# A recurrence's attention by halves of the batch, with its B and C projections as seven block products made with states on the partitions

## The chip, the cores and the metric

The kernel runs on one core of a Trainium2 chip, in one launch, in fp32. The metric is the device time of the whole kernel in microseconds (us), the lower the better. The core's engines work side by side and wait for each other through semaphores: TensorE (PE; its weight loads are listed as PEld), VectorE (DVE), ScalarE (ACT), GpSimd (POOL) and SyncE (SP), which here issues the transfers between DRAM and the on-chip memory SBUF. Matmuls write into PSUM, which has eight banks of 512 fp32 columns on 128 partitions.

## The reference

The kernel is a decoder of twelve stages over x of 4 sequences x 256 tokens x 256 channels. Each stage replaces x by the layer norm of x plus what the stage returns. The change lies in the seventh, a recurrence with 24 heads, 64 states and 64 channels per head (Di = 1536):

```python
x = hidden_states * rsqrt(mean(hidden_states ** 2, -1) + eps) * norm_w
xz = x @ in_proj_w.T + in_proj_b                  # 256 -> 2 x 1536
x, z = xz[..., :Di], xz[..., Di:]
x = silu(conv(x, conv_w) + conv_b)                # four taps, each channel by itself
xp = (x @ x_proj_w.T + x_proj_b).reshape(Bsz, L, H, 1 + 2 * S)
dt, Bs, Cs = xp[..., 0], xp[..., 1:1 + S], xp[..., 1 + S:]
Bs, Cs = (t / max(norm(t, axis=-1), 1e-12) for t in (Bs, Cs))
A_decay = exp(clip(A_log, -2.3, -0.01) * softplus(dt))
def step(carry, xs):                              # over the 256 tokens
    u_red = B_t * x_t.mean(-1)
    pe = mean(((1.0 - a_t) * u_red) ** 2, -1)
    boost = relu(tanh(beta * pe / (surprise_ema + 1e-06)))
    alpha = clip(alpha_base + (1.0 - alpha_base) * boost, 0.01, 0.999)
    h = alpha * h + (1.0 - alpha) * (B_t[..., None] * x_t[:, :, None, :])
    y = einsum('bhs,bhsd->bhd', C_t, h)
out = (Y * silu(z)) @ out_proj_w.T + out_proj_b   # 1536 -> 256
return hidden_states + res_gate * out
```

The eighth stage is a cross attention whose keys (`dca_keys`) do not depend on x; its queries (`dca_start`) do. The ninth rounds its weights, which `round_bits` does ahead of time in pieces.

## The kernel before

`run_ssd` (from L1281) computes the recurrence. A framework's scheduler turns the Python program into one queue per engine and sets the semaphores; an engine takes its instructions in the order of its queue, and a tile of a pool with n buffers comes free when its last reader has ended. `K.tt`, `K.ts`, `K.stt` and `K.reduce` are VectorE operations (L116, L125 and their neighbours), `K.ptt` is GpSimd's (L128), `K.act` ScalarE's (L131), `K.mm` TensorE's matmul (L137); `K.copy` takes VectorE and ScalarE by turns. An fp32 matmul is two passes in the profile's counts.

*In-projection* (`for f in range(2 * SDC)`). After the RMS norm and its transposes into `K.xT` (channels on partitions, 1024 tokens in columns), 24 chunks of 128 channels: two matmuls of 512 columns for each of two halves. Chunks 0 to 11 are copied by ScalarE into `xin`, with three columns of zeros ahead of each sequence, and convolved by VectorE: one `ts` and three `stt` of 128x1024, then SiLU into `xcT`. Chunks 12 to 23 go through SiLU into `YT`, the gates.

*Twelve pairs of heads.* `project(p)` makes B and C of a pair for eight tiles of 128 tokens: twelve matmuls each, with `xcT` as the stationary operand and 256 weight columns of `xw` moving. So tokens come out on partitions; VectorE adds the bias `xb` on the way from PSUM to `xp`. Pair 0 takes 24 columns more, the dt of all heads, from which `decays` makes `om`, one minus the decay. After each tile a step of the generator `attend(p - 1)` is put between, so that the attention of one pair lies between the products of the next:

- the squares of `xp` summed to `ss`, the reciprocal norms `rn`, the inputs transposed to `xt` (tokens on partitions), then some twelve small VectorE operations on `al` (alpha for 128 tokens x 16), and one tanh on ScalarE. GpSimd scales `xt` by (1 - alpha) x rn and the C half of `xp` by rn;
- alpha is transposed (`aT`), written to DRAM (`ad`) and read back on all partitions (`ap`, the buffer of `K.xT`): SP issues both;
- 16 transposes of `xp` (L1488) give BT and CT with states on partitions;
- for each two sequences, running products of alpha (`decay`, L1503, scans of 256 or 128 columns per sequence and head), scores C B^T (`sc`, `sd`), their product with the decays, values with `xt`, and the product with the gates in `YT`.

After each token tile one piece of `round_bits` goes between as well (`bits`).

*End.* `sums` (out-projection, twelve matmuls per token tile) of tiles 0 to 3 run beside the last pair's attention and `add` forms x; then come `dca_keys`, the sums of tiles 4 and 5, and `dca_start`, which has the sums and adds of tiles 6 and 7 put between its steps (`parts`).

Of the kernel before, what the change touches and what calls it, by code (L numbers as in the profile page):

```python
# [810 lines left out]
def small_heads_T(K, dst, src, col, chunks, scales=None, tp=None):  # L811


    ps = (tp or K.tp).tile([P, 4, P], F32, name="ps", tag="tp")
    for c in range(chunks):
        K.nc.tensor.transpose(ps[:, c, :], src[:, c * P : (c + 1) * P], K.ident)
    if scales is None:
        K.copy(dst[:, :, col : col + P], ps[:, 0:chunks, :])
    else:
        for lo, hi, g, b in scales:  # L820
            K.copy_scaled(dst[:, :, col + lo : col + hi], ps[:, 0:chunks, lo:hi], g, b)
# [451 lines left out]
def load_ssd(K, wp):  # L1273
    return {
        "cols": K.load(wp, "l2a_cols", [P, 86]),
        "rows": K.load_rows(wp, "l2a_rows"),
        "o": K.load(wp, "l2a_wo", [P, SDC, D], "(c p) n -> p c n", p=P),
    }


def run_ssd(K, w, more):  # L1281
    nc, tc = K.nc, K.tc
    N = B * L
    cols, rows = w["cols"], w["rows"]
    norm_w, in_b, conv_w, conv_b = cols[:, 0:2], cols[:, 2:26], cols[:, 26:74], cols[:, 74:86]
    dt_b, a_log, l2ab, l2beta, ema = (rows[:, SH * k : SH * (k + 1)] for k in range(5))
    out_b, res = rows[:, 120:376], rows[:, 376:377]
    by_b = lambda ap: ap.rearrange("p (b l) -> p b l", l=L)
    with ExitStack() as ctx:
        one = ctx.enter_context(tc.tile_pool(name="ssd1", bufs=1))  # L1290
        YT = one.tile([P, SDC, N], F32, name="YT")
        om = one.tile([P, NT, SH], F32, name="om")
        ab = one.tile([P, SH], F32, name="ab")
        nab = one.tile([P, SH], F32, name="nab")
        bse = one.tile([P, SH], F32, name="bse")


        cx = ExitStack()
        xcT = cx.enter_context(tc.tile_pool(name="ssdx", bufs=1)).tile([P, SDC, N], F32, name="xcT")
        with ExitStack() as c0:  # L1300
            c0.enter_context(K.turns())
            w0 = c0.enter_context(tc.tile_pool(name="ssd0", bufs=2))
            ws = c0.enter_context(tc.tile_pool(name="ssdw", bufs=6))
            pm = c0.enter_context(tc.tile_pool(name="ssdm", bufs=4, space=PSUM))
            xn = w0.tile([P, NT, D], F32, name="xn", bufs=1)
            ss = w0.tile([P, NT], F32, name="ss", bufs=1)
            for b in range(B):
# [5 lines left out]
                ps = K.tp.tile([P, DC, L], F32, name="ps", tag="tp")  # L1313
# [6 lines left out]
            for f in range(2 * SDC):  # L1320
                wi = ws.tile([P, DC, P], F32, name="wi")
                nc.sync.dma_start(out=wi, in_=K.A["l2a_in"][f])
                if f < SDC:
                    xin = w0.tile([P, B, L + 3], F32, name="xin")
                    nc.gpsimd.memset(xin[:, :, 0:3], 0.0)
                for h in range(2):
                    s = slice(512 * h, 512 * h + 512)
                    ps = pm.tile([P, 512], F32, name="ps")
                    for c in range(DC):
                        K.mm(ps, wi[:, c, :], K.xT[:, c, s], c == 0, c == DC - 1)  # L1330
                    if f < SDC:
                        K.act(xin[:, 2 * h : 2 * h + 2, 3 : L + 3], by_b(ps), AF.Identity, bias=in_b[:, f : f + 1])
                    else:
                        K.act(YT[:, f - SDC, s], ps, AF.Silu, bias=in_b[:, f : f + 1])
                if f < SDC:
                    acc = w0.tile([P, B, L], F32, name="acc")
                    cw = [conv_w[:, 4 * f + j : 4 * f + j + 1] for j in range(4)]
                    K.ts(acc, xin[:, :, 3 : L + 3], cw[3], conv_b[:, f : f + 1], MUL, ADD)
                    for j in range(3):
                        K.stt(acc, xin[:, :, j : j + L], cw[j], acc, MUL, ADD)  # L1340
                    K.act(by_b(xcT[:, f, :]), acc, AF.Silu)

        gb = one.tile([P, D], F32, name="gb")
        K.ts(gb, out_b, res, None, MUL)

        def sums(i, ps, lo, hi):
            for k in range(lo, hi):

                K.mm(ps, YT[:, k, i * P : (i + 1) * P], w["o"][:, k, :], k == 0 and i % 2 == 0, k == SDC - 1 and i % 2 == 1)
# [6 lines left out]
        with ExitStack() as c1:  # L1356
            c1.enter_context(K.turns(1))
            w1 = c1.enter_context(tc.tile_pool(name="ssda", bufs=1))
            w2 = c1.enter_context(tc.tile_pool(name="ssdb", bufs=2))
            ws = c1.enter_context(tc.tile_pool(name="ssdxw", bufs=3))  # L1360
            px = c1.enter_context(tc.tile_pool(name="ssdpx", bufs=2, space=PSUM))
            dram = c1.enter_context(tc.tile_pool(name="ssdad", bufs=2, space=bass.MemoryType.DRAM))
            pc = c1.enter_context(tc.tile_pool(name="ssdpc", bufs=1, space=PSUM))
            py = c1.enter_context(tc.tile_pool(name="ssdpy", bufs=1, space=PSUM))

            def decays(dt, wd):

                z = wd.tile([P, NT, SH], F32, name="z")
                e = wd.tile([P, NT, SH], F32, name="e")
                K.tt(z, dt, again(dt_b, NT), ADD)  # L1370
                K.act(e, z, AF.Abs)
                K.act(e, e, AF.Exp, scale=-1.0)
                K.act(e, e, AF.Ln, bias=K.eps[1.0])
                K.stt(z, z, 0.0, e, MAX, ADD)
                t = wd.tile([P, SH], F32, name="t")
                K.ts(t, a_log, -2.3, -0.01, MAX, MIN)
                K.tt(z, z, again(t, NT), MUL)
                K.act(z, z, AF.Exp)
                K.ts(om, z, -1.0, 1.0, MUL, ADD)
                K.ts(t, l2ab, -3.32, -0.015, MAX, MIN)  # L1380
                K.act(nab, t, AF.Exp, scale=LN2)
                K.ts(ab, nab, -1.0, 1.0, MUL, ADD)
                t = wd.tile([P, SH], F32, name="t")
                K.ts(t, l2beta, -2.0, 2.0, MAX, MIN)
                K.act(bse, t, AF.Exp, scale=LN2)
                t = wd.tile([P, SH], F32, name="t")
                K.ts(t, ema, 1e-6, None, ADD)
                nc.vector.reciprocal(t, t)

                K.stt(bse, bse, 1.0 / SD**3, t, MUL, MUL)  # L1390

            def project(p, rest=iter(()), beside=iter(()), bits=iter(())):


                n = 2 * P + (SH if p == 0 else 0)
                half = []
                for k in range(2):
                    xw = ws.tile([P, 6, n], F32, name="xw", padded_shape=[P, 6, 2 * P + SH])
                    nc.sync.dma_start(out=xw[:, :, 0 : 2 * P], in_=K.A["l2a_xw"][p, k])
                    if p == 0:  # L1400
                        nc.sync.dma_start(
                            out=xw[:, :, 2 * P : n],
                            in_=K.A["l2a_dt"][6 * P * k : 6 * P * (k + 1), :].rearrange("(c p) n -> p c n", p=P),
                        )
                    half.append(xw)
                xb = w2.tile([P, 2 * P], F32, name="xb")
                nc.sync.dma_start(out=xb, in_=K.A["l2a_xb"][p : p + 1, :].to_broadcast([P, 2 * P]))
                xp = w2.tile([P, NT, 2 * P], F32, name="xp")
                for i in range(NT):
                    ps = px.tile([P, 512], F32, name="ps")  # L1410
                    for k in range(SDC):
                        K.mm(ps[:, 0:n], xcT[:, k, i * P : (i + 1) * P], half[k // 6][:, k % 6, :], k == 0, k == SDC - 1)
                    K.tt(xp[:, i, :], ps[:, 0 : 2 * P], xb, ADD)
                    if p == 0:
                        nc.scalar.copy(dt[:, i, :], ps[:, 2 * P : n])
                    for _ in rest:
                        pass
                    next(beside, None)
                    next(bits, None)
                return xp  # L1420

            def attend(p, xp):

                hs = slice(2 * p, 2 * p + 2)

                ss = w2.tile([P, NT, 4], F32, name="ss")
                for h in range(2):
                    sq = w1.tile([P, 4, 4, SD], F32, name="sq")
                    v = xp[:, 4 * h : 4 * h + 4, :]
                    K.act(sq.rearrange("p i g s -> p i (g s)"), v, AF.Square)  # L1430
                    K.reduce(ss[:, 4 * h : 4 * h + 4, :], sq, ADD)
# [6 lines left out]
                for h in range(2):  # L1438
                    ps = K.tp.tile([P, 4, P], F32, name="ps", tag="tp")
                    for k in range(4):  # L1440
                        i = 4 * h + k
                        nc.tensor.transpose(ps[:, k, :], xcT[:, p, i * P : (i + 1) * P], K.ident)
# [1028 lines left out]
```

## Time and profile before

| | us |
|---|---|
| median of 3 runs (2395.62 to 2405.2) | 2399.39 |
| the profiled execution's own time | 2403.96 |
| its span, first to last instruction | 2402.2 |
| TensorE busy in it | 2227.1 (93%) |
| VectorE busy | 1461.9 (61%) |
| ScalarE busy | 787.2 (33%) |
| GpSimd busy | 260.4 (11%) |

The mean granted clock of TensorE was 0.947. The recurrence takes about a third of the span. By stretches, with the busy time of each engine:

| stretch (us) | what runs | length | PE | DVE | ACT | POOL |
|---|---|---|---|---|---|---|
| 1009.2 to 1055 | in-projection, convolved chunks | 45.8 | 42.57 | 41.75 | 27.36 | 0.99 |
| 1055 to 1101 | in-projection, gates | 46.0 | 44.93 | 15.09 | 24.13 | 0.22 |
| 1101 to 1704.7 | twelve pairs | 603.7 | 602.39 | 280.96 | 80.98 | 53.16 |
| 1704.7 to 1789.5 | keys, sums, begin of the queries | 84.8 | 82.02 | 53.15 | 17.82 | 16.63 |

A busy share is a mean over such stretches: what an operation costs depends on whether something waits for it where it stands. A row of the timeline shown below has the start in us, the duration in us, the engine, the line, the operation, output <- inputs, sizes (partitions x elements) and how many instructions it joins; square brackets hold the idle time ahead of it and what ended it. A row of a group has the busy time of all, the mean in ns of one, and the idle time ahead of them with what ended most of it.

### The profile page before, as it was taken

The page shows a single profiled execution, that of the slowest core. Times are in us where ns is not written, and L with a number is a line of the kernel's source. Part 1 is how long each engine was busy: PE and PEld are TensorE (multiplying, and loading weights), DVE is VectorE, ACT ScalarE, POOL GpSimd, SP SyncE. Part 2 cuts the span into 40 slices and gives each one's busy share as a digit, 9 for nine tenths or more (in the row PEclk, how much of TensorE's full clock was granted, in tenths as well). Part 3 has the DMA queues.
Part 4 walks back from the last instruction along what each step waited for, and adds up shares of the span by engine and source line. Part 5 has one row for each costly group of instructions (what it writes and reads, how often), then busy time and mean ns, then how long its engine had stood idle before and what let it go on. Part 6 is the DMA issues. An engine that isn't in the chain of part 4 may idle for free. (4 is left out here: it accounts for less than half of the span.)

```text
span 2402.2 us, 28595 instructions
## 1 busy us (share of the span) xinstructions
PE 2227.1 (93%) x10504; PEld 1516.5 (63%) x10504; DVE 1461.9 (61%) x3178; ACT 787.2 (33%) x1763; POOL 260.4 (11%) x419
## 2 busy tenths in 40 slices
PE   8899998589987999899999999999999988899998
PEld 4566763335434655536888888888776545477676
DVE  4999975999876121380465544445565658686466
ACT  5677765223432011261211111111122223253443
POOL 1000010220010322200101000110110001200001
PEclk9999998788987999999999999999998888999999
DMA  7222221222213644220222111111100021100000
GB/s 224 62 55 60 48 66 31 56 70 53 49 36 94 195 129 125 77 72 5 75 86 87 47 47 56 66 47 49 48 22 1 1 77 43 42 1 1 1 1 18
DMA packets 133747, 139.50 MB, mean 58 GB/s; under 512 B 13892, under 2 KB 121766, under 8 KB 131944
## 3 DMA queue, kind: packets, MB, share of 16 engines
q1 hardware_dynamic: 133608, 137.68, 20.0%
q8 instruction: 83, 1.36, 0.2%
q14 instruction: 56, 0.46, 0.1%
HBM read 134.79 MB, written 2.85 MB: 57 GB/s over the span
## 5 line engine op out<-in xcount | busy, mean ns | idle before, releaser
L137 PE MATMUL ps<-xw,xcT 128*128 128x256 f32 (+1 forms) x2304 | 518.9, 382 | 0.3 <-ACT YT L131 0.3
L137 PEld LDWEIGHTS ps<-xw,xcT 128*128 128x128 f32 x2304 | 430.8, 190 | 64.0 <-issue 1.9
L116 DVE TENSOR_TENSOR xp<-ps,xb 128x256 f32<-128x256 f32 x96 | 40.5, 422 | 232.1 <-PE ps L137 232.0
L137 PE MATMUL sc<-kT,qT 32*128 32x256 f32 (+2 forms) x768 | 167.5, 412 | 10.0 <-DVE qn L134 9.7
L131 ACT ACTIVATE dA<-delta,negA 128x255 f32<-128x255 f32 x256 | 118.5, 501 | 131.1 <-DVE s L535 129.4
L137 PE MATMUL ssmps<-s,idz 128*128 128x512 f32 x256 | 143.7, 670 | 17.1 <-DVE s L116 16.0
L535 DVE TENSOR_TENSOR_SCAN s<-dA,s 128x512 f32<-128x512 f32 x128 | 154.6, 1219 | 2.6
L137 PEld LDWEIGHTS sc<-kT,qT 32*128 32x128 f32 (+1 forms) x768 | 106.9, 204 | 73.4 <-issue 45.2
L116 DVE TENSOR_TENSOR hT<-u,a 128x512 f32<-128x512 f32 x48 | 33.2, 691 | 186.0 <-PE u L137 184.9
L131 ACT ACTIVATE sq<-xp 128x1024 f32<-128x1024 f32 x24 | 25.4, 1057 | 314.1 <-DVE xp L116 314.1
L174 POOL TENSOR_SCALAR rstd<-mv 128x2 f32<-128x2 f32 x48 | 11.6, 241 | 951.9 <-DVE mv L166 932.7
L134 DVE TENSOR_REDUCE qn<-sc 128x2 f32<-128x480 f32 (+1 forms) x192 | 87.2, 506 | 39.1 <-PE sc L137 38.1
L131 ACT ACTIVATE e<-sT 128x512 f32<-128x512 f32 x128 | 70.9, 590 | 112.0 <-PE sT L137 109.9
L137 PE MATMUL sT<-q,kT 32*128 32x256 f32 (+1 forms) x384 | 103.4, 518 | 3.4 <-ACT e L131 3.3
L1503 DVE TENSOR_TENSOR_SCAN dec<-xT,idz 128x256 f32<-128x256 f32 (+1 forms) x192 | 89.8, 537 | 19.0 <-DMA xT<-ad 19.0
L131 ACT ACTIVATE a<-g 128x512 f32<-128x512 f32 x48 | 28.7, 599 | 206.4 <-PE g L137 206.4
L137 PE MATMUL g<-xT,wj 128*128 128x512 f32 x192 | 92.1, 603 | 0.7 <-ACT rows L105 0.7
L137 PE MATMUL u<-xT,wj 128*128 128x512 f32 x192 | 90.9, 595 | 0.0
L137 PEld LDWEIGHTS y<-wj,hT 128*128 128x128 f32 x384 | 73.0, 190 | 26.6 <-issue 18.2
L116 DVE TENSOR_TENSOR s<-du,bc 128x512 f32<-128x512 f32 x128 | 87.7, 694 | 2.7 <-PE ssmps L137 2.5
L137 PE MATMUL ps<-xT,wi 128*128 128x512 f32 x192 | 85.7, 603 | 4.0 <-ACT xin L131 4.0
L137 PE MATMUL y<-wj,hT 128*128 128x256 f32 x384 | 89.2, 379 | 0.0
(504 smaller groups left out, 4057.4 us busy)
## 6 DMA issues: line engine op xcount, KB each, us to landing
bc<-bcd SPq DMA_DIRECT2D x128, 256.0 KB, 4.5
xw<-in_l2a_xw_dram SPq DMA_DIRECT2D x24, 768.0 KB, 4.9
xT<-ad SPq DMA_DIRECT2D x12, 1024.0 KB, 4.5
wj<-in_l1f_gate_dram SPq DMA_DIRECT2D x48, 128.0 KB, 2.9
wj<-in_l1f_up_dram SPq DMA_DIRECT2D x48, 128.0 KB, 2.8
wj<-in_l1f_down_dram SPq DMA_DIRECT2D x48, 128.0 KB, 3.0
sel<-cwd SPq DMA_DIRECT2D x32, 192.0 KB, 3.3
sel<-cwd SPq DMA_DIRECT2D x32, 128.0 KB, 3.2
```

The source lines that it names most:

```text
L116: self.nc.vector.tensor_tensor(out=out, in0=a, in1=b, op=op)
L131: self.nc.scalar.activation(out, in_, func, **kw)
L134: self.nc.vector.tensor_reduce(out=out, in_=in_, axis=AX.X, op=op, **kw)
L137: self.nc.tensor.matmul(out, lhsT=lhsT, rhs=rhs, start=start, stop=stop)
L174: self.nc.gpsimd.tensor_scalar(out=out, in0=in_, scalar1=add, scalar2=None, op0=ADD)
L535: nc.vector.tensor_tensor_scan(out=s.rearrange("p c l -> p (c l)"), data0=dA.rearrange("p c l -> p (c l)"), data1=s.rearrange("p c l -> p ...
L1503: nc.vector.tensor_tensor_scan(out=dec[:, k, h, :], data0=ap[:, h, at(bb, k, j) : at(bb, k, 2)], data1=K.idz[:, 0 : (2 - j) * P], initial=0.0,
```

## The change

`N` becomes 512: everything from the convolution to the out-projection is done for two sequences, then for the other two. `xcT` and `YT` are half as large.

B and C are made with states on partitions. Weights are now stationary and tokens (256 columns, a sequence) move. The output of a pair and half is a matrix of two row blocks (B, C) by two column blocks (the sequences), the inner dimension has two blocks of six chunks. In place of eight block products of six matmuls there are seven (Winograd's form): GpSimd makes four combinations of `xcT` once per half (`S`, in `convolved`) and four of the weights once per pair and half (`t0` to `t3`, in `combine`, one step after each of four products); the sums of products are taken as PSUM is evicted (`m1`, `u2`, `u5`, `u7`, `bc`). Weights of a pair are fetched in both halves, in four pieces.

With that the sixteen transposes go, and so do GpSimd's products with rn. The norms come from squares by matmuls with a matrix of ones (`sel`) and a second one (`pick`) that brings them to tokens on partitions. C's reciprocal norm goes with alpha through the transpose (`both`, L1522) and DRAM and comes back as `rc`, by which VectorE scales CT.

`tick` advances all attentions that are under way by one step after each product, and every third time there is one piece of `round_bits`, from the first half on. dt has its own matmuls (`decays`, 32 columns, partial sums folded by `fold`). ScalarE takes the first tap of the convolution. Between the halves: the twelve convolutions of the second half with the last attention steps between them, sums and adds of tiles 0 to 3, the gates of the second half. At the end `dca_keys`, now a generator, runs between the last attention's steps, then come the sums of tiles 4 to 7; `dca_start` keeps only the last adds as filler.

```diff
-    N = B * L
+    N = 2 * L
+    KC = SDC // 2
...
+        def tick(n=1):
+            for _ in range(n):
+                for g in list(live):
+                    if next(g, None) is None:
+                        live.remove(g)
+                if next(clock) % 3 == 0:
+                    next(bits, None)
...
+        def convolved(half, f):
+            ps = inputs(half, f)
+            xin = w0.tile([P, 2, L + 3], F32, name="xin")
...
+            K.act(acc, xin[:, :, 3 : L + 3], AF.Identity, scale=cw[3], bias=conv_b[:, f : f + 1])
+            for j in range(3):
+                K.stt(acc, xin[:, :, j : j + L], cw[j], acc, MUL, ADD)
+            K.act(by_b(xcT[:, f, :]), acc, AF.Silu)
+            if f >= KC:
+                k = f - KC
+                a11, a21, a12, a22 = (xcT[:, c, q] for c in (k, f) for q in seq)
+                K.ptt(S[:, 0, k, :], a21, a22, ADD)
+                K.ptt(S[:, 1, k, :], S[:, 0, k, :], a11, SUB)
+                K.ptt(S[:, 2, k, :], a11, a21, SUB)
+                K.ptt(S[:, 3, k, :], a12, S[:, 1, k, :], SUB)
...
+        def decays(half):
+            ps = bank()
+            for j in range(3):
+                for r in range(4):
+                    k = 3 * r + j
+                    K.mm(ps[32 * r : 32 * r + 32, :], w["dt"][:, k, :], xcT[:, k, :], j == 0, j == 2)
...
+        def fetch(p):
+            raw = ring.tile([P, 4, KC * P], F32, name="xw")
+            for k in (0, 1, 3, 2):
+                nc.sync.dma_start(out=raw[:, k], in_=K.A["l2a_xw"][p, k])
+            return raw
+
+        def combine(raw):
+            b11, b12, b21, b22 = (raw[:, k] for k in range(4))
+            t = []
+            for k in range(4):
+                t.append(big.tile([P, KC * P], F32, name=f"t{k}"))
+                K.ptt(t[k], (b12, b22, b22, b21)[k], (b11, t[0], b12, t[k // 3])[k], SUB)
+                yield
+            yield (b11, b21, b22, t[3], t[0], t[1], t[2])
+
+        def project(p, weights, following):
...
+            def product(wt, mov):
+                ps = bank()[:, 0:L]
+                for j in range(KC):
+                    K.mm(ps, wt[:, j * P : (j + 1) * P], mov(j), j == 0, j == KC - 1)
+                tick()
+                return ps
+
+            nc.scalar.copy(m1, product(b11, A(0, 0)))
+            K.tt(u2, product(t2, Sm(1)), m1, ADD)
+            K.tt(u5, product(t1, Sm(0)), u2, ADD)
+            next(following, None)
+            ps = product(t3, Sm(2))
+            K.stt(bc[:, 1, seq[1]], ps, bC, u5, ADD, ADD)
+            K.tt(u7, ps, u2, ADD)
+            next(following, None)
+            K.stt(bc[:, 0, seq[0]], product(b21, A(1, 0)), bB, m1, ADD, ADD)
+            next(following, None)
+            K.stt(bc[:, 1, seq[0]], product(b22, Sm(3)), bC, u5, ADD, ADD)
+            K.stt(bc[:, 0, seq[1]], product(t4, A(1, 1)), bB, u7, ADD, ADD)
+            next(following, None)
+            live.append(attend(p, bc))
+
+        def attend(p, bc):
...
+            K.act(sq, bc, AF.Square)
+            yield True
+            ps = K.tp.tile([P, N], F32, name="ps", tag="tp")
+            for r in range(4):
+                K.mm(ps[32 * r : 32 * r + 32, 0:L], sel, sq[:, r // 2, seq[r % 2]])
...
+                K.mm(out, sb[:, j * P : (j + 1) * P], pick, j == 0, j == 1)
...
+            nc.vector.tensor_copy(ss.rearrange("p k i h -> p (k i h)"), ps)
...
+            K.reduce(al, xt, ADD)
...
+            K.tt(al, al, again(bse[:, hs], 4), MUL)
+            yield True
+            K.act(al, al, AF.Tanh)
...
+            nc.vector.tensor_copy(both[:, 1].rearrange("p h i -> p i h"), rn[:, 1])
...
+            yield True
...
+            nc.tensor.transpose(ps, both.rearrange("p k h i -> p (k h i)"), K.ident)
+            aT = w2.tile([16, P], F32, name="aT")
+            nc.vector.tensor_copy(aT, ps)
+            ad = dram.tile([2, 2, N], F32, name="ad")
+            nc.sync.dma_start(out=ad.rearrange("k h (i t) -> (k h i) t", t=P), in_=aT)
+            ap = w1.tile([P, 2, N], F32, name="ap")
+            nc.sync.dma_start(out=ap, in_=ad[0].unsqueeze(0).to_broadcast([P, 2, N]))
+            rc = w1.tile([P, N], F32, name="rc")
+            for h in range(2):
+                nc.sync.dma_start(out=rc[64 * h : 64 * h + 64, :], in_=ad[1, h : h + 1].to_broadcast([64, N]))
...
+            BT, CT = bc[:, 0], bc[:, 1]
+            K.tt(CT, CT, rc, MUL)
+            decay(0, 0)
+            yield True
...
+        for half in range(2):
+            *_, weights = combine(raw)
+            decays(half)
+            for p in range(SDC):
+                following = iter(())
+                if p + 1 < SDC:
+                    following = combine(fetch(p + 1))
+                project(p, weights, following)
+                weights = next(following, None)
+            if half == 0:
+                raw = fetch(0)
+                for f in range(SDC):
+                    convolved(1, f)
+                    tick()
+                while live:
+                    tick()
+                out = [bank().rearrange("p (i n) -> p i n", n=D) for _ in range(2)]
+                for i in range(4):
+                    sums(i, out[i // 2][:, i % 2, :], 0, SDC)
+                for i in range(4):
+                    add(i, out[i // 2][:, i % 2, :])
+                for f in range(SDC):
+                    gates(1, f)
+                K.turn_pair(1)
...
+                for _ in dca_keys(K, w7, bank):
+                    tick()
...
-    a["l2a_xw"] = bc.transpose(0, 4, 6, 5, 2, 1, 3).reshape(SDC, 2, P, 6, 2 * P)
+    a["l2a_xw"] = bc.transpose(0, 4, 2, 6, 5, 1, 3).reshape(SDC, 4, P, 6 * P)
```

## The prediction

> **What bounds the kernel now.** I read the busy time by stretches first, then the timeline of each engine over one pair of heads, then groups by shape. The columns of the first line are stretch, length, busy time (and instructions) of PE, PEld, DVE, ACT, POOL, then clock and DMA.
>
> ```profile
> 1400.00:1450.00 50.00, 49.94 (x271) 42.22 (x272) 23.48 (x54) 5.74 (x9) 4.80 (x9) 1.00 0.14 50
> ...
> 1418.26 1.04 PE L1488 MATMUL ps<-idz,xp 128*128 128x128 f32 x8
> 1419.14 5.34 PE L137 MATMUL ps<-xw,xcT 128*128 128x256 f32 x24
> ...
> 1425.19 10.53 PE L137 MATMUL ps<-xw,xcT 128*128 128x256 f32 x48
> 1435.65 1.14 PE L137 MATMUL sc<-bc,bc 64*128 64x256 f32 x8
> 1436.62 0.61 PE L137 MATMUL sd<-bc,bc 64*128 64x128 f32 x8
> 1437.16 5.45 PE L137 MATMUL ps<-xw,xcT 128*128 128x256 f32 x24
> 1442.53 1.52 PE L137 MATMUL y<-dec,xt 128*64 128x256 f32 x16
> ```
>
> TensorE is never idle at full clock from 1100.8 to 1704.7 us: 603.9 us for twelve pairs, 50.3 each. One matmul is two passes; 48 passes take 1435.65 - 1425.19 = 10.46, so a pass is 0.218. A pair is 192 passes (41.9), scores and values twice (0.97 + 0.54 + 1.45, the differences of starts), 16 transposes of B and C (0.88 per eight) and about 1 for xcT and al. VectorE is busy 47% and GpSimd 10%, both off the path.
>
> The stage before it, and what shares the SBUF between VectorE and GpSimd:
>
> ```profile
> 1040.79 3.70 PE L137 MATMUL ps<-xT,wi 128*128 128x512 f32 x8 [0.63 <-ACT xin L131]
> ...
> 1042.22 3.79 DVE L125 SCALAR_TENSOR_TENSOR acc<-xin,w_l2a_cols,acc 128x1024 f32<-128x1024 f32 x3
> ...
> 611.61 1.26 POOL L128 TENSOR_TENSOR gate<-gate,u 128x512 f32<-128x512 f32 x1 [1.51 <-ACT gate L131]
> ...
> 611.99 1.44 DVE L116 TENSOR_TENSOR s<-du,bc 128x512 f32<-128x512 f32 x1
> ...
> 1152.52 3.25 POOL L128 TENSOR_TENSOR xp<-xp,rn 128x128 f32<-128x128 f32 x8 [91.04 <-DVE rn L1435]
> ...
> 1155.43 0.39 DVE L116 TENSOR_TENSOR al<-al,om 128x16 f32<-128x16 f32 x1
> ...
> 1155.86 0.19 DVE L116 TENSOR_TENSOR al<-al,rn 128x16 f32<-128x16 f32 x1
> ```
>
> The convolution (1040.79) is VectorE's: 4.43 per chunk, TensorE waiting 0.7. At 611.99 a VectorE operation on two SBUF tensors, 0.69 elsewhere, takes 1.44: it ends 0.56 after GpSimd's, so it ran after it. The 16-column operation at 1155.43 ends as GpSimd's run does (1155.77) and takes 0.39 in place of 0.19. So such pairs exclude each other. Operations that read PSUM do not show this. This decides my forecast.
>
> **The change, part by part.** I count from the first `wi` matmul (1009.2) to the last `wo` matmul (1789.5): 780 us.
>
> *Passes.* A pair and half was 96 passes and is 84: -12 x 0.218 = -2.6. Eight B and C transposes go: -0.9. Added: four 32-column norm matmuls, eight passes; the nearest row is
>
> ```profile
> L137 PE MATMUL o<-e,vt 128*32 128x256 f32 x512 | 39.5, 425 | 0.3 <-DVE oT L116 0.3
> L128 POOL TENSOR_TENSOR hT<-hT,sel 128x512 f32<-128x512 f32 x48 | 60.6, 1266 | 202.1 <-DVE hT L116 97.3 <-DMA sel<-cwd 91.4 <-DMA wj<-in_l1f_down_dram 7.8
> L128 POOL TENSOR_TENSOR t<-t,m 128x1024 f32<-128x1024 f32 x4 | 9.4, 2349 | 11.3 <-ACT m L131 11.3
> ```
>
> 39.5/512 = 0.077 each, 0.75 with the switch (1.74 if they don't overlap, at 0.218), and 0.4 for `pick`. Sum of a period: 84 x 0.218 = 18.3, xcT 0.49, `sel` 0.75, `pick` 0.4, al 0.15, scores 1.51, values 1.45: 23.05, against 25.15. Over 24 that alone is -50. Evicting on ACT and VectorE hides under the next product; with two banks and 2.61 per product there is less cover than the 5.2 of before.
>
> *The new wait.* In the changed program's order TensorE's `both` transpose stands after the fifth product, and everything of TensorE is queued behind it: the sixth and seventh products, the values, the next pair. It needs VectorE's chain of small al operations, which begins with the norms (`pick`, after the third product). GpSimd makes the next pair's weight combinations just then: t0 when the third product ends, t1, then t2 when the fourth (t3) ends. A 128x768 operation has no row; it lies between 1.27 (512 columns) and 2.35 (1024), and I take 1.82 from the line through both. Time zero is the end of the t3 product:
>
> GpSimd: t0 -2.8 to -1.0, t1 to +0.9, t2 to +2.75. VectorE: `ss` copy -2.3, ACT's root -2.0, the max fits at t0's end (-1.0), reciprocal -0.6; al x rn waits for t1's end (1.0); the rn copy for t2's (2.85); eviction of t3 0.45 (3.3); al squared 3.5; u7 3.9; two small ones 4.3; tanh 4.6 while the four score products with dec begin (0.63, 0.63, 0.37, 0.37 with one small between: 6.4); three small ones at 0.22: 7.05. TensorE arrives at 1.51 + 2.61 = 4.12. The wait is 3.0 in the second half of the batch, where this order holds. In the first, eviction comes ahead of al x rn: 2.5. I take 2.7, from the two. With 1.27 per combination it is 1.6, with 2.35 it is 4.5; without exclusion clip ends at 4.4 and the wait is 0.3.
>
> A page of the Trainium skill speaks to this: SBUF — State Buffer, Who interferes with whom, says that a VectorE instruction with two SBUF inputs, or a copy or tensor_scalar in a two-port mode, shares a port pair with GpSimd and the later one is held for the whole instruction. The rows show the first; for a small copy no row here decides. By the rule the rn copy is held (wait 3.0); by its nearest row, the reciprocal of one SBUF input that no row shows held, 0.6 less, 12 us in all.
>
> Behind the wait: aT, its DMA, then the next `xw` piece, which SP holds until the sixth product ends, then ap and rc (before: 4.5 to land 1 MB). They land at about 15; the values end at 13.9, YT to 14.7, scans (four 0.63, four 0.34) and CT x rc to 19.2, and on every second pair the xt copy to 19.9. The norm matmul wants it at 19.6: 0.3 every other time, 0.2 on average. So a period is 23.05 + 2.7 + 0.2 = 26.0. Per half: 18.3 for the first pair, 22 for the second, ten at 26: 300; in the first half about 4 more for the rounding pieces (three VectorE operations of 0.35 to 0.43 each, two or three pieces in five of the periods).
>
> *In-projection.* 96 passes of 512 columns at 0.438 (54 passes in 23.65, from 1011.8) are 42 a half, 45.8 now with VectorE's waits. ACT takes a tap, leaving 3 x 0.62 a chunk on VectorE, 22; but 24 GpSimd operations (0.72 by the 128x256 rows) exclude these two-input taps: some 18 fall between them, 13. VectorE ends at 35, TensorE two chunks earlier at 29 (two `xin` buffers), gates 21: 50.
>
> *Decay products.* 24 passes of 32 columns by 512; the row for 257 columns (64 in 5.8) doubled gives 0.18: 4.4, a copy 0.9, the fold 0.7: 6 a half, in place of 3.8 for 24 extra columns.
>
> *Between the halves.* TensorE has 21 (convolution) + 7 (last attention steps) + 21 (sums) + 21 (gates) + 1 = 71. VectorE must first do 22 of taps and some 20 of attention with 11 of exclusion; less what may follow, sums start at about 42 and not 28: 85.
>
> *End.* Before, 1704.7 to 1789.5 is 85. 21 of sums move out. The rest keeps its work (keys 19, sums 21, attention 8, queries 9), but sums stand behind the keys and the last values, and VectorE has 20 + 27 ahead of them: 47 + 21 = 68.
>
> Sum: 50 + 6 + 304 + 85 + 6 + 300 + 68 = 819, +39 on 780. The profiled execution took 2403.96 (span 2402.2), 4.6 above the median 2399.39 of the runs; its own sum is 2443, on the median **2438**.
>
> **Rivals.**
> *No exclusion on the chain* (GpSimd's operations short or late enough): wait 0.3, in place of 2.7, in 20 periods: -48; convolution -5, middle -10. 2438 - 63 = 2375, faster. For it: VectorE has room on average, 15 of 23. Against: three combinations stand back to back exactly at the chain. Chance 0.22; its range 2360 to 2387.
> *The chain is half freed* (combination 1.27, or fewer holds): wait 1.6 and the same edges but for 5: 2438 - 22 - 5 = 2411; around it, down to 2387, no difference that can be told. Chance 0.13.
> *The transfers become the bound.* Weights are read twice, 37.7 MB over 600 us or 63 GB/s; the page has slices at 195, so capacity speaks against. But ap stands behind an `xw` piece on SP. Landing 9 after issue in place of 4.5, the scans start 4 later and the xt copy or u2 holds TensorE by 3: +60, 2498. Chance 0.05.
> *The forecast*, 2411 to 2475: 0.6.
>
> **The numbers.** 0.5% is 12 us, about what a measurement tells from no change: faster below 2387, slower above 2411. Faster 0.22, same 0.13, slower 0.65. The range for eight in ten goes from 2378 (most of the faster case lies below and is left out) to 2475, the forecast with combinations near 2.1; its own is 2411 to 2475.
>
> **What would show it.** Right: TensorE's idle time before the L1522 transpose about 2.5 per pair, put down to VectorE; small al operations of 0.5 to 1.8 instead of 0.19 beside GpSimd's 128x768; pairs 26 apart. Wrong: pairs under 24.5 apart, the idle time elsewhere (the norm matmul, DMA), or combinations that take under 1.3.

## The result: 2.8% slower, and where the time went

The changed kernel takes 2469.37 us (median of 4 runs, 2467.43 to 2472.62) against 2402.3 for the kernel before on the same chip: a ratio of 1.0283, 95% interval 1.0253 to 1.0313. The profiled execution's span is 2468.8, 66.6 above that of before.

First the page of the changed kernel: its engines, and one of the two groups of GpSimd's weight combinations (the other 48 have a mean of 1824 ns).

```profile
PE 2217.4 (90%) x10388; PEld 1472.5 (60%) x10388; DVE 1572.3 (64%) x3483; ACT 855.6 (35%) x1874; POOL 447.0 (18%) x491
...
L128 POOL TENSOR_TENSOR t<-xw 128x768 f32<-128x768 f32 x48 | 87.6, 1825 | 242.8 <-PE ps L137 242.8
```

GpSimd is busy 187 us more than before; the 96 combinations at 1.82, the price of the forecast, take 175. TensorE is busy 9.7 less in the whole kernel. In the pairs alone it is 52.5 less (602.39 before, 279.19 + 270.71 in the rows below), close to the -50 of the forecast. Next the stretches of the changed kernel that answer to those shown of before (same columns); the first is 50 us in the middle of the second half's pairs, then all the pairs of each half:

```profile
1600.00:1650.00 50.00, 46.85 (x267) 37.88 (x268) 32.84 (x78) 10.19 (x15) 16.47 (x11) 1.00 0.28 96
...
1074.70:1380.30 305.60, 279.19 (x1499) 226.84 (x1500) 185.36 (x458) 61.18 (x91) 97.09 (x59) 0.97 0.31 97
1477.10:1765.50 288.40, 270.71 (x1497) 221.01 (x1498) 173.04 (x419) 61.07 (x90) 90.84 (x55) 1.00 0.26 85
```

TensorE, busy in 49.94 of 50 us before, now idles 3.15 of 50 at full clock. The 24 half pairs take 594.0 us; the twelve whole pairs took 603.9. So the pairs did become cheaper, by 10 us. The loss lies around them:

| from the first `wi` matmul | forecast | measured |
|---|---|---|
| in-projection, first half | 50 | 67.3 |
| decay products | 6 | 4.4 |
| pairs, first half | 304 | 305.6 |
| between the halves | 85 | 92.0 |
| decay products | 6 | 4.8 |
| pairs, second half | 300 | 288.4 |
| to the last `wo` matmul | 68 | 70.9 |
| sum (before: 780.5) | 819 | 833.4 |

That is +52.9. The stage begins 6.2 earlier (1003.0 in place of 1009.2): its first matmul starts 4.30 after the last one of the stage before, in place of 9.45, because with half the batch it waits for fewer norms (eight transposes of normalised tiles stand ahead of it in place of twelve); the rest is the stage before, which ended about 1 us earlier. What follows it takes 19.9 longer (632.4 against 612.5), for which the forecast had no term: 52.9 - 6.2 + 19.9 = 66.6.

The timeline of the changed kernel shows the wait of one pair in the second half:

```profile
1624.58 1.81 POOL L128 TENSOR_TENSOR t<-xw 128x768 f32<-128x768 f32 x1 [8.75 <-PE ps L137]
...
1625.33 1.08 DVE L120 TENSOR_SCALAR rn<-rn 128x16 f32<-128x16 f32 x1 [0.28 <-ACT rn L131]
1626.45 0.25 DVE L1499 RECIPROCAL rn<-rn 128x16 f32<-128x16 f32 x1
1626.46 1.80 POOL L128 TENSOR_TENSOR t<-xw,t 128x768 f32<-128x768 f32 x1
1626.73 1.56 DVE L116 TENSOR_TENSOR both<-both,rn 128x8 f32<-128x8 f32 x1
1627.46 1.58 PE L137 MATMUL sc<-bc 64*128 64x256 f32 x16
1628.21 0.16 DVE L1515 COPY both<-rn 128x8 f32<-128x8 f32 x1
1628.23 1.81 POOL L128 TENSOR_TENSOR t<-xw 128x768 f32<-128x768 f32 x1
1628.29 0.47 DVE L125 SCALAR_TENSOR_TENSOR bc<-ps,w_l2a_cols,u 128x256 f32<-128x256 f32 x1
1628.68 1.39 DVE L116 TENSOR_TENSOR both<-both 128x8 f32<-128x8 f32 x1
...
1633.26 0.27 PE L1522 MATMUL ps<-idz,both 128*16 128x128 f32 x1 [1.43 <-DVE both L122]
```

Three GpSimd combinations stand back to back, and three VectorE operations on 8 or 16 columns end within 0.1 us of the end of one of them: 1.08, 1.56 and 1.39 us where their equals take 0.17. TensorE waits 1.43 for the end of the chain. Over the stage its idle time ahead of this transpose is 33.0 us.

The same thing happens where I hadn't looked, in the norms at the very start of the stage (timeline of the changed kernel):

```profile
1003.42 1.80 POOL L128 TENSOR_TENSOR t<-xw 128x768 f32<-128x768 f32 x1
1003.49 2.21 DVE L122 TENSOR_SCALAR x<-x,mv,rstd 128x256 f32<-128x256 f32 x2 [1.13 <-POOL rstd L128]
...
1006.85 1.80 POOL L128 TENSOR_TENSOR t<-xw,t 128x768 f32<-128x768 f32 x1
1006.91 2.15 DVE L120 TENSOR_SCALAR YT<-x,ssn 128x256 f32<-128x256 f32 x2 [1.13 <-POOL ssn L128]
1008.95 1.09 PE L1351 MATMUL ps<-idz,YT 128*128 128x128 f32 x4 [4.12 <-DVE YT L120]
```

The program asks for the first pair's combinations after the gates, but the scheduler put them into GpSimd's queue as soon as their weights were there, among the roots of the norms. The normalising operation that takes 0.73 for two tiles takes 2.21, and TensorE waits 4.12.

### The profile page after: what moved, and what is told of

It reads as the page before. It is cut to its first block, busy times and chain, and to the rows that moved or that the text cites. A ratio compares the mean times of both kernels' runs of the same rounds, so it can differ in the third digit from the quotient of the medians.

```text
span 2468.8 us, 29249 instructions
## 1 busy us (share of the span) xinstructions
PE 2217.4 (90%) x10388; PEld 1472.5 (60%) x10388; DVE 1572.3 (64%) x3483; ACT 855.6 (35%) x1874; POOL 447.0 (18%) x491
## 5 line engine op out<-in xcount | busy, mean ns | idle before, releaser
L137 PE MATMUL ps<-S,t 128*128 128x256 f32 x864 | 203.7, 386 | 4.6 <-DVE u L116 4.6
L137 PEld LDWEIGHTS ps<-S,t 128*128 128x128 f32 x864 | 160.2, 191 | 33.1 <-issue 9.1
L137 PE MATMUL ps<-xcT,xw 128*128 128x256 f32 x576 | 136.3, 386 | 0.0
L128 POOL TENSOR_TENSOR t<-xw 128x768 f32<-128x768 f32 x48 | 87.6, 1825 | 242.8 <-PE ps L137 242.8
L1542 DVE TENSOR_TENSOR_SCAN dec<-ap,idz 128x256 f32<-128x256 f32 (+1 forms) x192 | 97.3, 558 | 33.7 <-DMA ap<-ad 32.4
L137 PEld LDWEIGHTS ps<-xcT,xw 128*128 128x128 f32 x576 | 106.2, 190 | 18.3 <-issue 3.1
L137 PE MATMUL ps<-xT,wi 128*128 128x512 f32 x192 | 92.6, 624 | 19.3 <-ACT xin L131 16.2
L128 POOL TENSOR_TENSOR t<-xw,t 128x768 f32<-128x768 f32 x48 | 87.5, 1824 | 101.3 <-issue 99.5
L125 DVE SCALAR_TENSOR_TENSOR bc<-ps,w_l2a_cols,u 128x256 f32<-128x256 f32 x72 | 34.3, 477 | 103.7 <-PE ps L137 103.7
L131 ACT ACTIVATE sq<-bc 128x1024 f32<-128x1024 f32 x24 | 25.4, 1057 | 211.6 <-DVE bc L125 211.6
```

Of the source, the lines that this page charges most:

```text
L125: self.nc.vector.scalar_tensor_tensor(out=out, in0=a, scalar=s, in1=b, op0=op0, op1=op1)
L128: self.nc.gpsimd.tensor_tensor(out=out, in0=a, in1=b, op=op)
L131: self.nc.scalar.activation(out, in_, func, **kw)
L137: self.nc.tensor.matmul(out, lhsT=lhsT, rhs=rhs, start=start, stop=stop)
L1542: nc.vector.tensor_tensor_scan(out=dec[j][:, k, h, :], data0=ap[:, h, at(k, j) : at(k, 2)], data1=K.idz[:, 0 : (2 - j) * P], initial=0.0, ...
```

## Experiments

Each is the changed kernel with the edit shown, in extracts; "before" ran beside them on the same chip.

**1. Combinations behind the alpha chain.** A one-column write into `t0` that reads the chain's last result makes GpSimd wait; t2 is formed from t1, so it follows. The program asks for the first three of them behind the fifth product and not one after each.

```diff
+                if k == 0 and ready:
+                    K.ts(t[0][:, 0:1], ready.pop()[:, 0, 0:1], 1.0, None, MUL)
-                K.ptt(t[k], (b12, b22, b22, b21)[k], (b11, t[0], b12, t[k // 3])[k], SUB)
+                a = t[1] if k == 2 else (b12, b22, b22, b21)[k]
+                K.ptt(t[k], a, (b11, t[0], b11, t[k // 3])[k], SUB)
...
-            next(following, None)
...
+            for _ in range(3):
+                next(following, None)
...
+            ready[:] = [t]
```

> The weight combinations of a pair are made to wait for the last small operation of the alpha chain, so GpSimd makes them after it. Theory A (GpSimd's weight combinations hold VectorE's operations on two SBUF inputs, and TensorE's transpose waits for the chain): the wait of 1.44 us ahead of the transpose falls below 0.3, pairs go from 24.85 to about 23.4 us, 23 pairs with a wait give 33 us, so 2469 becomes 2436 (2430 to 2445). Theory B (the chain is long by VectorE's own queue, the holds lie in its slack): the wait stays above 1, the time within 5 us of 2469.

Measured: 2439.74 us, ratio to before 1.015 (1.0103 to 1.0197), 30 us less than the changed kernel. Its timeline at the same place of a pair:

```profile
1607.81 0.17 DVE L120 TENSOR_SCALAR rn<-rn 128x16 f32<-128x16 f32 x1 [0.28 <-ACT rn L131]
...
1608.31 0.17 DVE L116 TENSOR_TENSOR both<-both,rn 128x8 f32<-128x8 f32 x1
...
1610.45 0.16 DVE L116 TENSOR_TENSOR both<-both 128x8 f32<-128x8 f32 x1
```

All three held operations are back at 0.17. Undisturbed pairs are 23.25 us apart in place of 24.85, and the idle time ahead of the transpose falls from 33.0 to 3.9. Theory A holds for the pairs, in mechanism and size: all of them together take 30.2 us less. Two more terms of this sum work against each other: the idle time ahead of the norm matmul grows from 7.4 to 13.4, and 10.2 us of the pairs run at half clock in place of 17.1.

**2. Eight products.** The same layout and halves, with no combinations and no sums of the inputs.

```diff
+            for n, (g, q) in enumerate(((0, 0), (1, 0), (0, 1), (1, 1))):
+                ps = bank()[:, 0:L]
+                for k in range(2):
+                    for j in range(KC):
+                        K.mm(ps, raw[:, 2 * k + g, j * P : (j + 1) * P], xcT[:, KC * k + j, seq[q]], j + k == 0, j + k == KC)
...
+                K.ts(bc[:, g, seq[q]], ps, x_b[:, 2 * p + g : 2 * p + g + 1], None, ADD)
```

> Halves, states on partitions and all else as in the changed kernel, but B and C as eight block products of six matmuls: no combinations of the weights, no sums of the inputs, GpSimd scales xt alone. Theory A: TensorE's work of 23.4 us a pair plus one product of 2.6 is 26.0 in place of 24.85, 24 pairs cost 28 us; the first norms and the convolutions, no longer held, give back about 20: 2477 (2465 to 2490). Theory B (holds cost nothing, the pairs are TensorE's work and VectorE's queue): 24.85 + 2.6 = 27.5 a pair, +63: 2532.

Measured: 2435.63 us, ratio 1.0127 (1.0072 to 1.0181). Both theories missed: more work on TensorE, and 34 us faster than the changed kernel. The pairs came as theory A had them (25.84 apart, forecast 26.0), but all pairs together cost only 6.5 us more than with seven products (600.5 against 594.0), because the changed kernel's first half has many pairs of 27 to 29.6. The edges gave more than thought: in-projection 56.9 (67.3), between the halves 82.1 (92.0), then 2.5 at the stage's end and 11.7 behind it, a part of which isn't this edit's (see *Behind the stage* below). In the changed kernel, then, the seventh product's saving does not pay for its combinations and sums.

**3. Edges freed.** The first pair's weights and the sums of the inputs wait for the last convolved chunk, again by small writes.

```diff
+            if p == 0:
+                K.ts(raw[:, :, 0], xcT[:, SDC - 1, 0:4], 1.0, None, MUL)
...
+            for n in (0, 2):
+                K.ts(S[:, n, :, 0], xcT[:, SDC - 1, 0:KC], 1.0, None, MUL)
```

> The pairs as in the changed kernel; the sums of the inputs and the first pair's weight combinations of each half are made to wait for the last convolved chunk. Theory A: the first norms (VectorE operations of 2.2 us in place of 0.74 beside a 128x768 combination) and the convolution's taps (0.94 in place of 0.62) are no longer held; the in-projection of the first half goes from 67 us to about 52, the stretch between the halves from 92 to about 85: 2469 becomes 2447 (2440 to 2455). Theory C (the convolutions are bound by the handing over of xin between ScalarE and VectorE): taps get shorter but chunks stay 2.8 to 3.4 us apart, less than 8 us gained.

Measured: 2470.42 us, ratio 1.0283 (1.0236 to 1.0331): nothing gained. The holds did go (a tap 0.756 in place of 0.938 on average, the in-projection 59.5, convolutions and sums between the halves 10.5 shorter), but the gates of the second half became 31.9 us long in place of 21.0. The timeline of this run shows why:

```profile
1424.94 0.30 DVE L166 BATCH_NORM_AGGREGATE mv<-stats 128x2 f32<-128x6 f32 x2
...
1437.32 1.80 POOL L128 TENSOR_TENSOR t<-xw,t 128x768 f32<-128x768 f32 x1
1439.08 0.22 POOL L174 TENSOR_SCALAR rstd<-mv 128x2 f32<-128x2 f32 x1
...
1440.13 0.73 DVE L122 TENSOR_SCALAR x<-x,mv,rstd 128x256 f32<-128x256 f32 x2 [14.89 <-POOL rstd L128]
1440.60 1.22 PE L192 MATMUL ps<-idz,x 128*128 128x128 f32 x4 [8.52 <-DVE x L122]
```

GpSimd also makes the roots of the norms. The statistics were there at 1425.24, the root began at 1439.08 behind the last of the moved operations, and TensorE idled 8.52. Neither theory had this: a hold on VectorE had been turned into a queue on GpSimd. By the rows of the profile some 7 us should be left as gain; its execution is the fastest of the four (2460.64, the others 2469.44 to 2471.72), so what took these 7 in the others isn't shown.

**4. Filler.** The sums of tiles 6 and 7 go back between the first queries of the next stage.

```diff
+            parts = [lambda i=i: sums(i, out[1][:, i % 2, :], 0, SDC) for i in (6, 7)]
...
+    parts[0]()
     next(q[0])
+    parts[1]()
```

> The sums of token tiles 6 and 7 go back between the first queries of the next stage, as in the kernel before; all else as in the changed kernel. Theory D (without that filler TensorE idles at the stage's end, and the granted clock, 0.70 for 60 us there against 0.79 before, falls with it): the stretch from the last out-projection to the first normaliser of the next stage shrinks, 8 to 12 us gained: 2459. Rival: VectorE's norms and reduces set the pace there and the clock drops as before, within 4 us of 2469.

Measured: 2460.22 us, ratio 1.0238 (1.019 to 1.0286), 9 less, with an interval that overlaps the changed kernel's (1.0253 to 1.0313). From the last out-projection to the next stage's first normaliser (the first matmul into `d`) it takes 50.5 us (60.8 in the changed kernel, 49.5 before). The stretches of the changed kernel, of this run, of the kernel before, and of run 1, which lacks the filler as the changed kernel does, each in its own fence:

```profile
1837.00:1897.00 60.00, 54.57 (x235) 36.95 (x233) 31.22 (x79) 10.62 (x17) 4.20 (x7) 0.70 0.07 23
```

```profile
1843.50:1894.00 50.50, 46.46 (x224) 32.02 (x222) 28.52 (x75) 9.07 (x15) 3.78 (x6) 0.78 0.08 27
```

```profile
1790.00:1839.00 49.00, 46.48 (x220) 32.36 (x214) 28.04 (x73) 8.88 (x14) 3.77 (x6) 0.79 0.08 28
```

```profile
1811.70:1867.10 55.40, 49.67 (x242) 33.74 (x241) 31.76 (x82) 10.61 (x17) 4.68 (x8) 0.80 0.07 24
```

With the filler back, TensorE's busy time and the clock (0.78) are those of before. But the low clock of the changed kernel (0.70) does not come from the missing filler: runs 1 to 3 lack it too and take 53.9 to 55.4 us here at a clock of 0.80 to 0.82. Against them the filler shortens the stretch by 3.4 to 4.9. A part of that is only moved: counted from the end of the pairs to the same normaliser, it is 123.7 us with the filler, 131.8 in the changed kernel, and 123.7 to 127.9 in runs 1 to 3. And of the 9.9 us between the two profiles 6.5 lie behind the normaliser, in code that the edit doesn't touch. So theory D isn't shown: the clock does not follow the filler, and what the filler is worth in the whole stays open.

**5 and 6. Seven freed, and eight with the filler.** Number 5 joins 1, 3 and 4, with one repair: in the second half the later sums and the first pair's weights wait for the norms of tiles 0 to 3, so that the roots come first. Number 6 is 2 with 4.

```diff
+                raw = fetch(0, K.x[:, 3, :])
+                combined(2, K.x[:, 3, :])
                 for f in range(SDC):
                     gates(1, f)
```

> Three edits together: the pairs' weight combinations wait for the alpha chain, the first pair's combinations and the sums of the inputs wait for the last convolved chunk (in the second half the later part of them for the norms of tiles 0 to 3, whose roots GpSimd makes), and the sums of tiles 6 and 7 go between the first queries. Theory A: 30 us from the pairs as measured alone, some 20 from the edges (in-projection 57 and the stretch between the halves 82, as with eight products), 9 from the filler: 2469 - 59 = 2410 (2402 to 2420). Rival, that freeing the edges moves the wait to a place behind them as the run of that edit alone suggests: 2430.

> Eight products as before in this layout, with the sums of tiles 6 and 7 between the first queries. Theory A: the eight products have no hold to be freed from, so only the filler's 9 us come off 2436: 2427, and seven freed products beat eight by about 17 (pairs of 23.3 and 25.84, 24 of them 61 us, less what the combinations still cost elsewhere). Rival, that seven products do not pay in this kernel even when freed: the two runs are within 5 us of each other or eight is ahead.

Measured: seven freed 2414.43 us, inside theory A's range, ratio 1.0046 (1.0022 to 1.007); eight 2441.24, ratio 1.0163 (1.0129 to 1.0198). With the roots ahead of them, the moved operations do no harm: in run 5 the in-projection takes 59.7 us (67.3 in the changed kernel), the stretch between the halves 85.0 (92.0) and its gates 24.5 (31.9 in run 3). By the medians the edges give 16 beyond the 39 of experiments 1 and 4. Once freed, seven products beat eight by 27 us; in the changed kernel they lost to them by 34. The forecast was 2427 for the eight and a lead of 17. In the eight products' total the filler did nothing here (2436 in run 2, 2441 now), though the stretch behind the last out-projection did shrink, from 55.3 to 50.6; it came back in the stretch before (74.0 against 68.4).

**7. The next wait.** The timeline of run 5 shows what now ends last in some pairs:

```profile
1655.08 2.75 DVE L1552 TENSOR_TENSOR_SCAN dec<-ap,idz 128x256 f32<-128x256 f32 x5 [3.39 <-DMA ap<-ad]
...
1658.98 0.67 DVE L103 COPY xt<-ps 128x512 f32<-128x512 f32 x1
...
1659.80 0.64 PE L137 MATMUL ps<-sq,w_l2a_pick 128*32 128x256 f32 x8 [3.02 <-DVE xt L103]
```

On every second pair VectorE copies xt, behind scans that wait for alpha's transfer; the norm matmul needs the PSUM buffer that the copy empties. In run 5 this adds up to 15.6 us of idle time.

```diff
-            K.copy(xt.rearrange("p i h d -> p i (h d)"), ps)
+            nc.scalar.copy(xt.rearrange("p i h d -> p i (h d)"), ps)
```

> As the run with three edits together (2414), and the copy of the transposed inputs xt goes from PSUM always by ScalarE. Theory A: with the holds gone, what ends last ahead of the norm matmul is VectorE's xt copy of every second pair, behind scans that wait for alpha's transfer (15.6 us of TensorE's idle time in the profile of that run); on ScalarE it is early, most of the 15.6 goes: 2404 (2400 to 2408). Rival: ScalarE's squares and table loads now come later and the norm matmul waits for them: 2410 to 2416.

Measured: 2398.58 us, ratio 0.9968 (0.9942 to 0.9993), 16 less than run 5 and a little below the forecast range; the rival is out. Of the 15.6 us of idle time 0.7 is left. The clock may have had a part in the rest: 10.2 us of run 5's pairs ran at half clock, none of this run's. Its stretches over the pairs of the two halves:

```profile
1069.00:1346.00 277.00, 270.14 (x1502) 221.74 (x1503) 159.63 (x463) 63.92 (x96) 93.64 (x57) 1.00 0.32 102
1437.00:1707.00 270.00, 269.23 (x1499) 221.82 (x1498) 138.54 (x422) 64.01 (x95) 90.41 (x55) 1.00 0.28 89
```

TensorE is busy 269.23 of 270 us in the second half, nearly every pair 23.25 apart, and the clock is full in both. This is the first version ahead of the kernel before, by 0.3% (0.1 to 0.6).

**8. Rounding.** Run 7, and the 36 rounding operations wait for the norms between the halves: a small write into the tile of its factors reads the normalised x.

```diff
     inv = pool.tile([P, 3], F32, name="biti")
+    K.ts(inv, K.x[:, 3, 0:3], 1.0, None, MUL)
     nc.vector.reciprocal(inv, K.mean)
```

> As the run before it in this list, and the rounding of the ninth stage's weights (36 VectorE operations of 0.35 to 0.43, 14 us) is made to wait for the norms between the halves, so that it lies beside the second half's gates and first pair and not in five pairs of the first half. Theory A: the first half's pairs take 289 us against 276.5 of the second, most of the difference by these operations: 8 us gained, 2396, under the kernel before. Rival: the difference is the granted clock's (half speed at times in the first half only), or the operations are held beside GpSimd's sums at the gates: no gain, 2404 or more.

Measured: 2399.68 us, ratio 0.9982 (0.9961 to 1.0003), not to be told from run 7. The pairs of the first half do fall from 276.8 to 270.6, now all close to 23.25, but the second half's take 273.8 (269.9) and its gates 28.3 (26.9). Theory A's 8 us didn't come: the rounding costs some 6 in the first half, and moved, it costs most of that elsewhere. The 12.7 us by which run 5's first half was longer than its second were 6.9 in run 7. These 5.8 aren't the xt copy's alone: the idle time behind it was 8.3 in the first half of run 5 and 6.6 in the second, and 10.2 us of the first half ran at half clock there, none in run 7. So the rival's clock had a part in it.

## Why the prediction was right, and where it wasn't

The direction and the range (2378 to 2475) held; the point was 31 us low.

- **TensorE's work of a pair, 23.05.** Freed of waits it is 23.25 in runs 1, 5 and 7. Right.
- **Decay products, 6.** 4.4 and 4.8: the 24 passes took 2.8 in place of 4.4, because they start by fours within 0.02 us of each other, 0.45 after the four before.
- **The wait ahead of the transpose, 3.0 in the second half and 2.7 on average.** The mechanism is shown by experiment 1, the size was half: 1.43. The step that failed is "the rn copy for t2's end (2.85)". The copy ran in 0.16 us at 0.8 after the end of the t3 product, as t2 was just beginning, so the eviction of t3 followed at 0.85 and not at 2.85; what was held till t2's end was al squared, whose two inputs lie in SBUF. From there the chain went as worked out, and the transpose began at 5.8 in place of 7.05, while TensorE arrived at 4.37 (forecast 4.12). Over all pairs 33.0 us against some 54.
- **The rule of the page and its row.** By the page SBUF — State Buffer of the Trainium skill (Who interferes with whom) a tensor_scalar or a copy in a two-port mode is held too, though it reads one SBUF tensor. The trace agrees for tensor_scalar (1.08 in place of 0.17 at 1625.33, 2.21 in place of 0.73 at 1003.49). For the copy it depended on the moment. In 16 of the changed kernel's 24 pairs it was issued 0.01 or 0.02 us ahead of t2 and took 0.16; in the other eight it met no combination that went on, and took the same. In run 4 the last pair's copy was issued 0.09 after a GpSimd operation had started, and took 0.70:

```profile
1781.73 2.12 POOL L128 TENSOR_TENSOR x<-x,r_l2x_bo 128x256 f32<-128x256 f32 x3 [4.52 <-DMA r_l2x_bo<-in_l2x_bo_dram]
...
1781.82 0.70 DVE L1515 COPY both<-rn 128x8 f32<-128x8 f32 x1
```

So this one copy was held as the rule says, and what the prediction had wrong was the moment. The reciprocal took 0.24 to 0.26 everywhere in the pairs, also when it was issued 0.11 or 0.19 after a combination's start (1528.31, 1292.46).

- **The xt copy, 0.2 a pair.** 7.4 us of idle time ahead of the norm matmul in 24 pairs, 0.3. Right while the other wait covered it; freed of that, it grew to 15.6.
- **Pairs of the first half, 304.** 305.6, but not for the reasons given, so this is luck: the waits were smaller, the rounding dearer than the 4 us allowed (6.2 by run 8), and 17.1 us of these pairs ran at half clock. In the whole stage it was 47.8, against 7.0 before.
- **In-projection, 50.** 67.3: the largest miss. The forecast let VectorE begin the taps with the first matmul and end them at 35, and gave TensorE another 15 behind that. The timeline of the changed kernel has the first six and the last 24 of the half's 36 taps:

```profile
1018.55 4.11 DVE L125 SCALAR_TENSOR_TENSOR acc<-xin,w_l2a_cols,acc 128x512 f32<-128x512 f32 x6 [3.55 <-ACT acc L131]
...
1029.83 25.01 DVE L125 SCALAR_TENSOR_TENSOR acc<-xin,w_l2a_cols,acc 128x512 f32<-128x512 f32 x24 [0.17 <-ACT acc L131]
```

From the first `wi` matmul (1002.84) the taps begin at 15.7 and end at 52.0, and 15.3 follow. So nearly the whole miss is the late begin, which the sum put at nothing: the norms of the other two sequences now come behind the first matmul, with the first pair's combinations among them. In run 2, without combinations, the taps begin at 11.2 and the in-projection takes 56.9; so the combinations and sums cost 10.4. Some 5 us of the late begin aren't lost: they are the stage's earlier start. That the taps' own length came out is luck: free they take 0.755 each in place of 0.62, and the holds on them cost 0.2 each and not the 13 us of the sum.

- **Between the halves, 85, and end, 68.** 92.0 and 70.9; 82.1 and 68.4 without sums and combinations.
- **Behind the stage, nothing.** +19.9, of which some 11.3 lie ahead of the next stage's first normaliser (60.8 against 49.5). The prediction described that the filler leaves the first queries and priced only its own 21 us of work; by runs 1 to 3 its absence costs 4.4 to 5.9 there, and the rest goes with the low clock of this one profile. The others, 8.7, lie behind that normaliser, 571.7 against 563.0, with code that no edit touches and as many matmuls; the granted clock is 0.91 against 0.94. The eight profiles of edited kernels show 565.2 to 565.9 there at 0.92 or 0.93 (five) or 571.7 to 572.3 at 0.91 (three); why the one or the other isn't settled.
- **The rivals.** The "half freed" case had the right wait (1.6) and 2411 as its time, because it kept the low prices of the edges. That transfers bind was wrong: alpha's transfer landed in 4.7 us (4.5 before). "No exclusion" is refuted by the timeline and experiment 1.

So the time came out inside the range partly by errors against each other: too much for the waits in the pairs, too little for the edges, which halving the batch makes twice, and nothing for what follows the stage.

## What to carry to other kernels

Work that is given to an idle GpSimd isn't free while VectorE has a chain on the way to TensorE: look at every place where a scheduler that fills queues by readiness may put it, not only where the program asks for it, and tie it with a dependency to a stretch in which VectorE has nothing urgent. A loop that is split in two pays its fill and drain twice, so price the edges from their own rows before the saving per turn. And when a wait is removed, look at the next one in the new trace: here moving one copy gave as much as freeing the edges, and only then was the saving there.

## What was unexpected of the hardware

A short VectorE operation can get between two GpSimd operations that stand back to back: in the timeline of the pair the copy begins at 1628.21 and the next combination at 1628.23, both run at their usual length, and the operation after it is held 1.39 us. The same copy, issued 0.09 us behind GpSimd's start, took 0.70 (run 4). GpSimd paid little for the holds: 89 of the 96 combinations took 1.80 to 1.83 us in the changed kernel, 86 in run 1.

TensorE's clock drops to one half in stretches of 3.41 us and whole multiples of it (6.83, 10.24, 13.65, 20.48, 23.89 and 34.13 in the changed kernel), but for a last one that ends with the execution. The longest from this stage on, 23.89 from 1844.3, follows gaps in TensorE's work among the queries (1.38 us ahead of 1842.43, 0.91 ahead of 1845.08), where the filler used to be. Runs 1 to 3 have the same gaps, and the clock was at half there for 13.65, 13.65 and 10.24 us; so the gaps alone don't set the length. The page TensorE: Matmul & The Clock Gate of the Trainium skill (Part 1, The HAM clock gate) gives a window of about 3.4 us over which activity is judged, and the trace agrees with the length.
